# Chunk 0 and the tail of a recurrent-plus-experts kernel: some stores, a pair of sums, the later steps of three cells and three weight loads change place in an order written by hand

## The chip, the cores and the metric

The kernel runs on one core of a Trainium2 chip. A core has five engines that run side by side: TensorE (PE in the profile; its weight loads have a row of their own, PEld), VectorE (DVE), ScalarE (ACT), GpSimdE (POOL) and SyncE (SP), which here only issues transfers (DMAs). Each engine takes its own instructions strictly in the order in which the program issued them, so an instruction that has to wait holds up all that stand behind it on that engine. The metric is the time of one execution in microseconds (us), as the median of several runs; less is better.

## The reference, cut to what matters

The input x has 8 x 1024 tokens of 512 numbers, all float32. One layer is computed:

```
xn = layernorm(x)                                    # 8192 x 512
# a gated linear recurrence over the 1024 tokens of each sequence
hidden, forget, input = split(xn @ W1 + b1, 3)       # 1024 wide each
diff  = softplus(-forget) - softplus(-input)
h_t   = sigmoid(diff) * g(hidden_t) + sigmoid(-diff) * h_(t-1)   # the reference in logs: cumsum, cumlogsumexp
s     = h @ W2 + b2
# feed-forward: one shared expert, and one of 32 routed experts for each token
shared = (silu(xn @ sg) * (xn @ su)) @ sd
e      = argmax(xn @ gate_w);  score = sigmoid(max(xn @ gate_w))
routed = (silu(xs @ G[e]) * (xs @ U[e])) @ D[e]      # xs = xn * score, inner width 1024
out    = x + s * silu(shared + routed)
```

Here g(z) is z + 0.5 for z of at least 0 and sigmoid(z) below.

## The kernel before, in words

**Two stages.** The first stage goes over the tokens in 16 chunks of 512 and computes the recurrence, the shared expert and the choice of expert. What belongs to a token is written to two tables in memory: `rec1` holds xn times score, `rec2` holds x, the recurrence's output and the shared expert's output. The second stage goes over the 32 experts, gathers each expert's tokens from these tables, computes the routed expert and stores the result.

**Products by Strassen's scheme.** A chunk has 20 jobs (`JOBS`): for four pairs of column blocks the projections f, i, h (forget, input, hidden) of the recurrence and g, u (gate, up) of the shared expert. Each job is a product of a 512 x 256 weight block with the 512 tokens of the chunk, made of seven half-size products P1 to P7 (`multiply`, line 762 holds the matmul) instead of eight. For that it needs four sums of weight blocks, S1 to S4 (slots 0 to 3 of the tile `sums`), and four sums of token blocks (`t_sum`). P5 uses S1, P6 uses S2, P7 uses S3, P3 uses S4. S2 = S1 - A11 and S4 = A12 - S2 depend on each other; S3 = A11 - A21 stands alone. In chunk 0 (jobs 0 to 19) the sums are computed by `combine`, S1 and S4 on GpSimdE (lines 641 and 645), S2 and S3 on VectorE (lines 643 and 647), and then `save` (line 650) stores them to memory, 512 KB for each job. Later chunks only fetch them again (line 656). The tile `sums` has three buffers, `natural` (the weight block itself, loaded at line 594) has four.

**Banks.** P5 starts in a PSUM bank that ScalarE copies out (tag `p5`, line 776); P3 then adds onto the same bank, four places later. In the same way P6 adds onto P1's bank after P1's copy, P7 after P6's and P4 after P7's, each five places later. P2's bank and P5's bank are two that change roles from job to job. The copies are ScalarE instructions at lines 776 and 778, and pairs of them are added (`join`, line 788) by VectorE or GpSimdE.

**An order written by hand.** The first stage runs under a manual schedule. `now` counts slots; one slot issues one of the seven products of the current jobs, in the order P1, P4 of two jobs before, P5, P7 of the job before, P2, P6, P3. Everything else is put down with `at(slot, ...)` and is issued when the counter comes to that slot, after the slot's product. A slot is therefore a place in each engine's queue, not a time. From chunk 1 on, the products of the chunk before with W2 and sd (line 1058, "fills") are put between the others; chunk 0 has none.

**Cells.** A `Cell(c, p)` takes the f, i, h of one pair and does the elementwise part of the recurrence in 17 steps: absolute values, exponentials and logarithms on ScalarE (slots 24 to 31 after the job's start), `difference`, `less` and `more` on VectorE (32 to 34; lines 840, 844, 848), two gates on ScalarE (36 and 37; line 851, which need what `more` wrote), `sigmoid` and `positive` (39, 40), `value`, `weighed` and two scans on VectorE (42 to 47). There are four cells for each chunk.

**The second weights.** `out_sum` forms four sums of the weights W2 and of sd on VectorE (line 954) and stores each to a place in memory called `tdram` (line 958); `out_fetch` loads these or the plain blocks for the fills (lines 988 and 991).

**Prep.** For each chunk `Prep` loads x, normalises it, and `scale` (line 560) multiplies by the score; its store to `rec1` is line 561.

**The hand-over.** After the last product of the last chunk only its fills are left, 112 of them, two for each P1 to P7 and column half: this is the tail. `Dispatch` has by then made a table of which token goes where. In the tail the integer table `idx` is written, `numbers` loads the table again in two halves of four small transfers (line 1340), and VectorE turns each half into row numbers (line 1341) from which the later gathers of the experts start. The first expert's three weight blocks of 2 MB, e_wg, e_wu and e_wd, are loaded by `chunks[0].weight` (line 193): "g" ahead of the tail, "u" after 12 of its slots and "d" after 28. All these transfers stand in SyncE's one queue, and the built program gives them eight semaphores in turn, so that a transfer is issued only when the one eight places ahead of it has landed.

Of the kernel before, what the change touches and what calls it, by code (L numbers as in the profile page):

```python
# [17 lines left out]
P = 128  # L18
# [15 lines left out]
def tile_kernel(  # L34
# [45 lines left out]
    nc = tc.nc  # L80
# [24 lines left out]
    rec1 = dram.tile([N + 1, H], FP, name="rec1")  # L105
    rec2 = dram.tile([N + 1, 3 * H], FP, name="rec2")

    def work(name):
# [11 lines left out]
        out=upper, in_=ones, pattern=[[1, P]], compare_op=ALU.is_gt, fill=0.0,  # L120
# [42 lines left out]
    def expert(where):  # L163
        e = nc.values_load(
            where, engines=[ET.SP], min_val=0, max_val=E - 1,
            skip_runtime_bounds_check_because="the numbers of experts, or a count of them, clamped",
        )
        return [w[bass.ds(e, 1)].rearrange("o a b -> (o a) b") for w in (rgate_w, rup_w, rdown_w)]
# [207 lines left out]
    def alloc2(shape, tag, name):  # L376
# [4 lines left out]
    chunks = [  # L381
        Chunk(
            alloc2, alloc_w, f"e{e}",
            lambda t, e=e: pools["idx"][:, e * CT + t : e * CT + t + 1],
            lambda t, b, e=e: pools["fours"][:, b, e * CT + t : e * CT + t + 1],
            WIDTHS[e], lambda e=e: expert(eid[0:1, e : e + 1]), e == 0, e == E - 1,
        )
        for e in range(E)
    ]
# [3 lines left out]
    NP = DI // (2 * P)  # L393
# [32 lines left out]
    now = 0  # L426
    steps = {}

    def at(slot, what, *args):
        assert slot >= now  # L430
        steps.setdefault(slot, []).append(lambda: what(*args))
# [3 lines left out]
    class Prep:  # L435
# [121 lines left out]
        def scale(self, t):  # L557
            i = self.c * NT + t
            xn = self.xs.pop(t)
            nc.vector.tensor_scalar(xn, xn, self.sc[:, t : t + 1], None, ALU.mult)  # L560
            at(now + 2, lambda: nc.sync.dma_start(out=rec1[i * P : (i + 1) * P, :], in_=xn))

        def plan(self, g):

            g += 50 if self.c == 1 else 0
            for t in range(NT):
                at(g + 2 + 2 * t, self.load, t)
                at(g + 16 + 2 * t, self.stats, t)
                at(g + 32 + 2 * t, self.normal, t)
                at(g + 35 + 2 * t, self.store, t)  # L570
                at(g + 43 + 2 * t, self.pieces, t)
                at(g + 50 + 2 * t, self.turn, t)
                late = 70 if self.c == NCHUNK - 1 else 0
                at(g + 72 + late + 2 * t, self.again, t)
                at(g + 86 + late + t, self.scale, t)
            at(g + 12, self.keep)
            at(g + 24, self.variance, 0, NT)
            at(g + 28, self.spread, 0, NT)
            at(g + 66, self.router)
            at(g + 72, self.logits)  # L580
            at(g + 76, self.choose)
            at(g + 80, self.score)
# [77 lines left out]
    for n in range(NJOB):  # L660
        if n >= 3:
            at(7 * (n - 2) + 2, load, n)
        if n >= JC:
            at(7 * (n - 2) + 4, fetch, n)
        else:
            for q, s in ((0, 1), (2, 3), (1, 5), (3, 8)):
                at(7 * max(n - 1, 0) + s, combine, n, q)
            at(max(7 * n + 4, 10), save, n)

    tsum = {}  # L670

# [140 lines left out]
    class Cell:  # L812
# [66 lines left out]

        def plan(self):  # L880
            g = SC * self.c + 7 * JOBS.index((self.p, "f"))
            for slot, what, *args in (
                (24, self.size, "f", "d"), (25, self.exp, "lf"), (26, self.size, "i", "m"),
                (28, self.exp, "li"), (29, self.log, "lf"), (31, self.log, "li"),
                (32, self.difference), (33, self.less), (34, self.more),
                (36, self.gate, "i", 1.0), (37, self.gate, "f", -1.0),
                (39, self.sigmoid), (40, self.positive),
                (42, self.value), (43, self.weighed), (45, self.scan, 0), (47, self.scan, 1),
            ):
                at(g + slot, what, *args)  # L890

    class Hidden:

# [41 lines left out]
    def out_tile(name):  # L935
        return op.tile([P, NP, HC], FP, tag="wo", name=name, bufs=3)
# [10 lines left out]
    def out_sum(half, q):  # L947
        B11, B12, B21, B22 = out_blks[half][:4]
        l, r = {
            1: lambda: (B12, B11), 3: lambda: (B22, B12),  # L950
            2: lambda: (B22, out_blks[half][4]), 4: lambda: (B21, out_blks[half][5]),
        }[q]()
        o = out_tile(f"ot{half}_{q}")
        nc.vector.tensor_tensor(o, l, r, ALU.subtract)
        if q in (1, 2):
            out_blks[half].append(o)
        d = tdram[half, q] = dram.tile([P, NP * HC], FP, name=f"tdram{half}_{q}")
        at(now + 3, lambda: nc.sync.dma_start(out=d[:, :], in_=o.rearrange("p q f -> p (q f)")))

    for half, (a, b) in enumerate(((6, 18), (14, 40))):  # L960
        for k in range(4):
            at(a + 2 * k, out_load, half, *divmod(k, 2))
        for k, q in enumerate((1, 2, 4, 3)):
            at(b + 5 * k, out_sum, half, q)
# [6 lines left out]
    def out_fetch():  # L971

        u, name = next(out_next, (None, None))
        if u is None:
            return
        half = u[1]
        if "far" in pools:
            turn = next(far_turn)
            if turn % 5 < 2:
                o = pools["far"].tile([P, NP, HC], FP, tag="far", name=f"far{turn}")  # L980
            else:
                o = out_tile(f"w{name}_{half}")
            out_w[u, name] = o
        else:
            o = out_w[u, name] = out_tile(f"w{name}_{half}")
        if name in ("P1", "P2", "P3"):
            k, m = {"P1": (0, 0), "P2": (1, 0), "P3": (1, 1)}[name]
            nc.sync.dma_start(out=o, in_=out_block(half, k, m))
        else:
            q = {"P5": 1, "P6": 2, "P7": 3, "P4": 4}[name]  # L990
            nc.sync.dma_start(out=o.rearrange("p q f -> p (q f)"), in_=tdram[half, q][:, :])
# [20 lines left out]
    for c in range(NCHUNK):  # L1012
        g = SC * (c + 1)
        fast = c == NCHUNK - 1
        for p in range(NP):
            for q in range(1, 5):
                if p == NP - 1:
                    slot = (1, 2, 4, 6)[q - 1]
                else:
                    slot = (110, 112, 122, 132)[q - 1] + p - SC  # L1020
                at(g + slot, out_combine, c, 0, q, p)
                if fast:
                    slot = (20, 22, 26, 30)[q - 1] + p // 2
                else:
                    slot = (42, 44, 52, 61)[q - 1] + p
# [356 lines left out]
    d = Dispatch()  # L1382
# [36 lines left out]
    def due(slot):  # L1419

        c, s = divmod(slot, SC)
        if c == 0:
            return 0
        s -= 1
        if c == NCHUNK:
            return int(2 * (c - 1) * PER + min(max(RATE * s, 0), 2 * PER))
        part = min(max(s / 62, 0), 1) + min(max((s - 62) / 74, 0), 1)
        return int((2 * (c - 1) + part) * PER)
# [3 lines left out]
    for now in range(END):  # L1432
        name, back = ORDER[now % 7]
        n = now // 7 - back
# [25 lines left out]
    pools["far"] = c1.enter_context(tc.tile_pool(name="far", bufs=2, side="right"))  # L1460
    for _ in range(2):
        out_fetch()
    chunks[0].weight("g")
    k = 0
    while filled < 2 * NCHUNK * PER:
        now += 1
        for step in steps.pop(now, ()):
            step()
        while filled < due(now):
            next(fill)  # L1470
            filled += 1
        k += 1
        if k in (12, 28):
            chunks[0].weight("ud"[k // 28])
        if filled >= 2 * NCHUNK * PER - 24 and "xsT" not in vars(chunks[0]):
            pools["work"] = ps_w
            for t in range(CT):
                chunks[0].transpose(t)
# [50 lines left out]
    with tc.tile_pool(name="wo", bufs=3) as wo, tc.tile_pool(name="so", bufs=3) as so:  # L1529
        n = nc.values_load(  # L1530
            nov[0:1, 0:1], min_val=0, max_val=MAXOV,
            skip_runtime_bounds_check_because="a sum of at most MAXOV comparisons of counts that sum to N",
        )
# [56 lines left out]
```

## Time and profile before

| | |
|---|---|
| median of 3 runs | 4281.0 us (4280.41 to 4290.57) |
| the profiled execution itself | 4241.17 us |
| its span, first to last instruction | 4239.4 us |
| mean granted TensorE clock | 0.997 |
| TensorE busy | 4191.6 us, 99% |
| VectorE, ScalarE, GpSimdE busy | 2108.4, 1998.3, 1105.1 us |
| moved by DMA | 925.63 MB, 218 GB/s on average |

The profile shows one execution. Its timeline view lists instructions of an engine with start, length, line, output and inputs; a bracket at the end says how long the engine stood idle before, and which instruction of which engine ended that wait. The view of waits sums the same by pairs. Tensors carry the names of the program without buffer numbers. SPq is SyncE's queue of transfers.

### The profile page before, as it was taken

The numbers are of one execution on the slowest core, as the hardware profiler recorded it, in microseconds if no ns is written. First come the engines' busy times: TensorE is split into PE (matmuls) and PEld (weight loads), VectorE is DVE, ScalarE is ACT, GpSimd is POOL, SyncE is SP. The second block draws the span as 40 slices with busy tenths as digits, with TensorE's granted clock in tenths as the row PEclk, the third lists the DMA queues.
The fourth block names the chain that finished last, engine by engine and source line by source line (L and its number), as shares of the span: only waits on it lengthen the run. The fifth ranks groups of instructions, "written<-read, shape, count | busy, mean of one in ns | idle before, by whom it ended". The sixth has DMA issues, their size and how long they took to land.

```text
span 4239.4 us, 52532 instructions
## 1 busy us (share of the span) xinstructions
PE 4191.6 (99%) x18923; PEld 3568.1 (84%) x18923; DVE 2108.4 (50%) x3483; ACT 1998.3 (47%) x3662; POOL 1105.1 (26%) x1171
## 2 busy tenths in 40 slices
PE   8999999999999999999999999999999999999998
PEld 6888888888888888888888888866777788889998
DVE  6646454554554545555554456424444444544444
ACT  5676676666676767667666666500111111111111
POOL 3322112121221122212211125342232333333221
PEclk9999999999999999999999999999999999999999
DMA  7776666676676766766666666585666667677773
GB/s 261 234 225 224 214 218 212 204 230 209 210 223 210 227 207 206 229 210 215 216 211 220 207 191 199 168 290 178 213 225 224 210 233 243 220 252 244 242 264 114
DMA packets 507240, 925.63 MB, mean 218 GB/s; under 512 B 38397, under 2 KB 325021, under 8 KB 498786
## 3 DMA queue, kind: packets, MB, share of 16 engines
q1 hardware_dynamic: 479394, 832.27, 59.4%
q0 software_dynamic: 27584, 89.98, 6.4%
q8 instruction: 151, 2.47, 0.2%
q14 instruction: 111, 0.91, 0.1%
HBM read 805.27 MB, written 134.92 MB: 222 GB/s over the span
## 4 chain that ended last, share of the span: by engine, by line
PE 95%; DVE 2%; ACT 1%; issue 1%; DMA 1%; SPq 0%; POOL 0%; POOLq 0%; DVEq 0%; ACTq 0%
PE b L762 24%; PE u L1058 18%; PE c L762 12%; PE e_g L272 11%; PE e_u L272 11%; PE acc L261 11%; PE a L762 6%; PE b L713 0%; PE lgp L521 0%; DMA wP<-tdram 0%; DVE d L848 0%; DVE h L873 0%; DVE d L840 0%; PE lgt L531 0%; PE b L728 0%
## 5 line engine op out<-in xcount | busy, mean ns | idle before, releaser
L762 PE MATMUL b<-t,sums 128*128 128x256 f32 x2536 | 651.2, 379 | 2.2 <-DVE t L682 1.5
L1058 PE MATMUL u<-wP,s 128*128 128x256 f32 x2032 | 596.3, 379 | 2.4 <-issue 2.0
L277 ACT ACTIVATE e_sig<-e_g 128x280 f32<-128x280 f32 (+15 forms) x256 | 101.8, 398 | 933.4 <-PE e_g L272 933.3
L762 PEld LDWEIGHTS b<-t,sums 128*128 128x128 f32 x2536 | 480.6, 190 | 68.6 <-issue 1.9
L272 PE MATMUL e_g<-e_xsT,e_wg 128*128 128x296 f32 (+15 forms) x2048 | 518.0, 396 | 0.0
L272 PE MATMUL e_u<-e_xsT,e_wu 128*128 128x296 f32 (+15 forms) x2048 | 518.0, 396 | 0.0
L261 PE MATMUL acc<-e_h,e_wd 128*128 128x296 f32 (+15 forms) x2048 | 512.7, 396 | 0.0
L272 PEld LDWEIGHTS e_g<-e_xsT,e_wg 128*128 128x128 f32 x2048 | 389.1, 190 | 87.1
L272 PEld LDWEIGHTS e_u<-e_xsT,e_wu 128*128 128x128 f32 x2048 | 389.2, 190 | 87.0
L261 PEld LDWEIGHTS acc<-e_h,e_wd 128*128 128x128 f32 x2048 | 389.2, 190 | 87.0
L1058 PEld LDWEIGHTS u<-wP,s 128*128 128x128 f32 x2032 | 385.8, 190 | 57.0 <-issue 5.0
L279 DVE TENSOR_TENSOR e_sig<-e_sig,e_g 128x280 f32<-128x280 f32 (+15 forms) x256 | 113.3, 442 | 482.6 <-ACT e_sig L277 482.2
L762 PE MATMUL c<-xnT,sums 128*128 128x256 f32 x1268 | 326.8, 380 | 13.9 <-ACT p L776 13.5
L762 PE MATMUL b<-t,nat 128*128 128x256 f32 x1268 | 327.5, 381 | 0.0
L762 PE MATMUL b<-xnT,nat 128*128 128x256 f32 x1268 | 327.5, 381 | 0.0
L762 PE MATMUL c<-t,sums 128*128 128x256 f32 x1268 | 326.1, 380 | 0.0
L762 PE MATMUL a<-xnT,nat 128*128 128x256 f32 x1268 | 325.5, 379 | 0.1
L213 POOL DMA_INDIRECT e_xs<-rec,fours x276 | 261.8, 949 | 179.9 <-DMA e_rest<-rec,idx 80.2
L360 POOL DMA_INDIRECT out_dram<-e_rest,idx x84 | 93.2, 1110 | 801.8 <-DVE e_rest L359 798.9
L762 PEld LDWEIGHTS c<-xnT,sums 128*128 128x128 f32 x1268 | 240.3, 190 | 49.9 <-issue 14.0
L762 PEld LDWEIGHTS b<-t,nat 128*128 128x128 f32 x1268 | 242.6, 191 | 33.4
L762 PEld LDWEIGHTS b<-xnT,nat 128*128 128x128 f32 x1268 | 242.0, 191 | 33.5 <-issue 0.5
(245 smaller groups left out, 6298.9 us busy)
## 6 DMA issues: line engine op xcount, KB each, us to landing
sums<-sdram SPq DMA_DIRECT2D x300, 512.0 KB, 4.8
nat<-in_L_attn_W_dram SPq DMA_DIRECT2D x192, 512.0 KB, 4.6
e_wg<-L_ffn_routed_gate_w_dram SPq DMA_DIRECT2D x32, 2048.0 KB, 8.4
e_wu<-n_L_ffn_routed_up_w_dram SPq DMA_DIRECT2D x32, 2048.0 KB, 11.3
e_wd<-L_ffn_routed_down_w_dram SPq DMA_DIRECT2D x32, 2048.0 KB, 19.0
wP<-tdram SPq DMA_DIRECT2D x127, 512.0 KB, 4.3
nat<-L_ffn_shared_gate_w_dram SPq DMA_DIRECT2D x64, 512.0 KB, 4.7
nat<-n_L_ffn_shared_up_w_dram SPq DMA_DIRECT2D x64, 512.0 KB, 4.4
```

Source lines behind the costliest of these rows:

```text
L213: nc.gpsimd.indirect_dma_start(out=r[:, b, :], out_offset=None, in_=rec1.rearrange("n (a d) -> (n a) d", a=NA), in_offset=bass.IndirectOff ...
L261: nc.tensor.matmul(accs[m][:, :W], lhsT=wd[:, j, m * P : (m + 1) * P], rhs=h[:, :W], start=(j == 0), stop=(j == NI - 1),)
L272: nc.tensor.matmul(o[:, :W], lhsT=w[:, k, j * P : (j + 1) * P], rhs=xsT[:, k, :W], start=(k == 0), stop=(k == KH - 1),)
L277: nc.scalar.activation(sig[:, :W], g[:, :W], AF.Sigmoid)
L279: nc.vector.tensor_tensor(sig[:, :W], sig[:, :W], g[:, :W], ALU.mult)
L360: store = nc.gpsimd.indirect_dma_start(out=of[:, :], out_offset=bass.IndirectOffsetOnAxis(ap=col[:n, :], axis=0), in_=o, in_offset=None, b ...
L762: nc.tensor.matmul(ps, lhsT=lhs[:, k, :], rhs=rhs[:, k, :], start=(new and k == 0), stop=(k == KQ - 1),  skip_group_check=True,)
L1058: nc.tensor.matmul(ps[:, q, :], lhsT=lhs[:, q * P : (q + 1) * P], rhs=w[:, p, :],  start=(q == 0 and p == 0 and name in ("P1", "P2", "P5") ...
```

## The change

Six places of the hand-written order change; no instruction is added or taken away, and the products of TensorE keep their order.

- The store of `scale` to `rec1` is issued six slots after the multiplication instead of two (all chunks).
- In chunk 0, S2 is formed two slots earlier, S4 two slots earlier and ahead of S3, which comes five slots later; `save` is issued three slots later.
- The steps of cells 0 to 2 of chunk 0 that come after slot 31 (from `difference` on) are put two slots later. Cell 3 of chunk 0 and all later chunks keep their slots.
- The stores to `tdram` are issued nine slots after the sum instead of three.
- In the tail, the first expert's "g" weights are asked for after 10 slots instead of ahead of it, "u" after 20 instead of 12, "d" after 32 instead of 28. In the built program "g" then stands behind all eight transfers of `numbers`, and "d" behind one more store of the last results.

```diff
         def scale(self, t):
...
-            at(now + 2, lambda: nc.sync.dma_start(out=rec1[i * P : (i + 1) * P, :], in_=xn))
+            at(now + 6, lambda: nc.sync.dma_start(out=rec1[i * P : (i + 1) * P, :], in_=xn))
...
-            for q, s in ((0, 1), (2, 3), (1, 5), (3, 8)):
+            for q, s in ((0, 1), (1, 3), (3, 6), (2, 8)):
                 at(7 * max(n - 1, 0) + s, combine, n, q)
-            at(max(7 * n + 4, 10), save, n)
+            at(max(7 * n + 7, 13), save, n)
...
         def plan(self):
             g = SC * self.c + 7 * JOBS.index((self.p, "f"))
+            late = 2 if self.c == 0 and self.p < NP - 1 else 0
             for slot, what, *args in (
...
             ):
-                at(g + slot, what, *args)
+                at(g + slot + (late if slot > 31 else 0), what, *args)
...
-        at(now + 3, lambda: nc.sync.dma_start(out=d[:, :], in_=o.rearrange("p q f -> p (q f)")))
+        at(now + 9, lambda: nc.sync.dma_start(out=d[:, :], in_=o.rearrange("p q f -> p (q f)")))
...
     for _ in range(2):
         out_fetch()
-    chunks[0].weight("g")
     k = 0
     while filled < 2 * NCHUNK * PER:
...
         k += 1
-        if k in (12, 28):
-            chunks[0].weight("ud"[k // 28])
+        if k in (10, 20, 32):
+            chunks[0].weight("gud"[k // 10 - 1])
```

## The prediction

> **What bounds the kernel now.** I read the page first, then TensorE's waits, then the timelines of the places where it waits, then the order of the instructions in the two builds. The page:
>
> ```profile
> PE 4191.6 (99%) x18923; PEld 3568.1 (84%) x18923; DVE 2108.4 (50%) x3483; ACT 1998.3 (47%) x3662; POOL 1105.1 (26%) x1171
> ```
>
> TensorE is the bound nearly everywhere, so only stretches where it stands still can give time back. They lie in chunk 0 and at the hand-over to the experts. TensorE's waits of the first 220 us (total, times, longest), then lines of its timeline there (start, length; the wait before it in brackets):
>
> ```profile
> PE c L762 <- ACT p L776: 13.5, 7, 3.4
> PE b L762 <- DVE sums L643: 0.6, 2, 0.4
> PE c L762 <- POOL sums L645: 0.4, 1, 0.4
> ```
>
> ```profile
> 55.94 1.03 PE L762 MATMUL b<-t,sums 128*128 128x256 f32 x4
> 60.36 1.66 PE L762 MATMUL c<-xnT,sums 128*128 128x256 f32 x4 [3.40 <-ACT p L776]
> 61.81 1.91 PE L762 MATMUL b<-xnT,nat 128*128 128x256 f32 x4
> ...
> 76.62 1.10 PE L762 MATMUL c<-xnT,sums 128*128 128x256 f32 x4 [2.24 <-ACT p L776]
> ...
> 119.19 1.10 PE L762 MATMUL c<-xnT,sums 128*128 128x256 f32 x4 [1.65 <-ACT p L776]
> ...
> 155.09 1.10 PE L762 MATMUL c<-xnT,sums 128*128 128x256 f32 x4 [1.92 <-ACT p L776]
> ```
>
> The product waiting is always P3, four slots behind P5 in the same bank, held until ScalarE has copied P5 out. A product of four records starts every 0.865 us (43.36 to 44.22). Against that pace the gaps cost: 2.30 (at 50.7), 3.56 (60.4), 2.40 (76.6), 1.17 (102 to 104, two waits for sums), 1.19 (111.3), 1.82 (119.2), 1.33 (146.9), 2.09 (155.1). After three of them the records take 1.9 instead of 1.0: half clock for about 3.4 us, 1.75 each (155.09 to 160.30 is 5.21 for four products, 3.46 at pace). With 0.1 at 84.6 that is 21.2 us.
>
> The gaps are of two kinds. At 50.7, 76.6, 111.3 and 146.9 ScalarE is busy without a break: two exponentials, a table load of 1.28, a logarithm of 1.15, then the copy. At 60.4, 119.2 and 155.1 it stands before a gate (line 851) that waits for VectorE, with the copy queued behind. ScalarE, then VectorE:
>
> ```profile
> 54.04 1.28 ACT L851 ACT_TABLE_LOAD   x1
> 58.90 1.06 ACT L851 ACTIVATE i<-d 128x1024 f32<-128x1024 f32 x1 [3.58 <-DVE d L848]
> 59.87 0.35 ACT L776 COPY p<-c 128x256 f32<-128x256 f32 x1
> ```
>
> ```profile
> 51.98 1.22 DVE L840 TENSOR_TENSOR d<-d,m 128x1024 f32<-128x1024 f32 x1 [2.34 <-ACT m L836]
> ...
> 55.13 1.74 DVE L954 TENSOR_TENSOR ot<-wo,wo 128x1024 f32<-128x1024 f32 x1
> ```
>
> VectorE idles 2.34 before line 840, then runs other work between 840 and 848. At the hand-over (SyncE's waits, then TensorE's and VectorE's timelines):
>
> ```profile
> SPq L1340 <- DMA e_wg<-L_ffn_routed_gate_w_dram: 5.6, 1, 5.6
> ```
>
> ```profile
> 2769.43 3.69 PE L1058 MATMUL u<-wP,s 128*128 128x256 f32 x16 [0.37 <-DMA wP<-tdram]
> 2775.14 3.69 PE L1058 MATMUL u<-wP,s 128*128 128x256 f32 x16 [2.02 <-issue]
> ```
>
> ```profile
> 2772.68 0.41 DVE L1341 TENSOR_SCALAR fours<-number,piece 128x372 int32<-128x372 f32 x1 [1.26 <-DMA number<-table]
> 2773.01 1.42 DVE L1010 TENSOR_TENSOR s<-sh,s 128x256 f32<-128x256 f32 x4
> 2774.35 0.68 DVE L1070 TENSOR_TENSOR o<-u,a 128x512 f32<-128x512 f32 x1
> ```
>
> The 2 MB of e_wg, issued at 2753.94, hold up the numbers; VectorE waits for these, so line 1070 empties its bank only at 2775.03, and P5 starts at 2775.14. At a unit's pace of 3.46 the two gaps cost 0.53 and 2.25, together 2.78.
>
> **The change, part by part.** *Cells 0 to 2 of chunk 0, later steps two slots on.* Nothing is added. In the new order P5's copy and P7's eviction stand ahead of the table load and the gate, so P3 no longer waits for VectorE; P2's copy and P6's eviction are now behind the gate, with five slots' grace instead of four. In cell 0, VectorE does the ot of line 954 in its idle 2.34 (its inputs are there, and the store that frees its buffer leaves about 39.5 as before). Then, from 52.25, when the copy of P2 is out: join, 840, 844, join, cast, difference, 848. Those seven take 4.7 us start to start alone and 6.8 if each runs beside GpSimdE (0.42 becomes 0.95 and 1.21 becomes 1.74 in this trace); I take 5.8, which gives the gate at 58.1 instead of 58.90. TensorE wins 3.56 there, but ScalarE still owes the same work: from the gate on it needs 5.9 us of starts (0.97 for a big one, 0.25 to 0.36 for an eviction) to cell 1's first step, which begins at 64.0 instead of 67.02, and from there to P3 it is 9.6 us as now. So the 76.6 gap grows and 3.0 us remain. Cell 1's gate costs nothing now and little then (my count puts its P3 0 to 0.4 late). In cell 2 the copy of P5 is out 2 us early, nothing else is late by five slots: 1.8 gained.
>
> *S4 ahead of S3 (20 combinations of each kind).* No instruction more. Cell 3's steps are not moved, but one subtraction (0.34 start to start) leaves the place between lines 840 and 844, and S4 on GpSimdE, which began at 150.01 right behind it and lay beside two VectorE instructions (0.53 each), comes earlier. That is 0.3 to 1.4 off the gate's wait; I take 1.1, leaving a gap of about 1.0. The waits for sums (1.17) go too, at no gain: in the same cell ScalarE's unbroken chain sets P3's start, and the 1.19 at 111.3 becomes 2.36.
>
> *The clock.* The 1.92 gap in cell 3 was followed by half clock, 1.75; no gap of 1.65 or less in this trace was. Here a rule speaks against me: the Trainium skill, "TensorE: Matmul & The Clock Gate", Part 1, has the clock halve only after an idle window of about 3.4 us. By it neither 1.92 nor 2.24 could have halved it, and a shorter gap in cell 3 would save nothing more (sum 8.7). The rows of 1.9 us behind both gaps are there, so I go by them; but a gap of 2.14 at 50.7 was not punished, so the phase of a window matters, and a new half-clock stretch of 1.75 may appear in cell 2, where the gap grows to about 2.2.
>
> *Stores issued later: 20 saves of 512 KB, 8 tdram stores of 512 KB, 64 rec1 stores of 256 KB.* Same number, same bytes. SyncE now finds most of them ready: waits of 26 (line 650), 25 (958) and 14 us (561) in the first 250 us go, and loads queued behind leave up to 4 us sooner. TensorE waits for none of those loads (no nat in its list), so I book zero. The cover is their lead: load of job n at slot 7n-12, first product at 7n. From below, an earlier load could help the idle 1.35 before line 647 at 49.22, already counted as idle; from above, the sums ring, next paragraph but one. In chunk 1 three x loads now stand behind rec1 stores and wait for a landing (4.9 median); behind them is a load with 12 slots to spare, about 15 us.
>
> *Tail.* e_wg, e_wu, e_wd (three transfers of 2 MB) move behind the eight numbers, the last one also behind a store that waits for line 1081. Numbers then land by about 2766, line 1070 runs when P2 ends at 2769.1, and both gaps go: 2.78, taken as 2.8. What is late next: e_wd, issued about 2785.7 instead of 2775.55 and needed at 2797.8. The page's e_wg, alone in its queue, lands in 8.4; so 3.7 us of cover, and each us beyond costs one. GpSimdE's gathers are not moved.
>
> Sum: 3.0 + 1.8 + 1.1 + 1.75 + 2.8 = 10.45, say 10.5. The profiled execution took 4241.2 (span 4239.4); so 4230.7 for such a one. The median of the runs is 4281.0, 39.8 above, which no view explains; I take the saving over unchanged: 4270.5, 0.25% less. About 0.3%, 12.8 us, is what a measurement of this kernel can tell from no change.
>
> **The rivals.**
> *The gates run dry.* VectorE meets no GpSimdE work: cell 0's gate at 57.2 (4.1 gained, not 3.0), cell 3's as soon as its table is loaded at 151.4 (2.2, not 1.1), and the longer gap in cell 1 splits over P7, P2 and P3 so that its half clock goes too (1.75). 14.4 gained: 4266.6. For it: the copies that blocked are provably out of the way. Against: GpSimdE's S4 and S1 do fall between 52 and 56.
> *ScalarE takes it back.* Cell 0's gate at 58.9 as now: 1.9 left at P3 of cell 1; cell 3 unchanged; a new half clock in cell 2 (minus 1.75 from 1.8). With the tail 4.75: 4276.2.
> *Slower: the ring of three sums.* S1 of job n writes the buffer that save n-3 reads. Saves go three slots later and S2 two earlier, so from save to S2 there are 10 slots instead of 15: 8.65 us less S1's 0.9, so 7.8. If a save takes longer, S2 blocks VectorE, then the gates and joins. Each us beyond, over 14 jobs, is up to 14 us: slower than before from a lag plus landing of about 8.6, by over 0.3% from 9.5. Example at 10: 31 lost, 20 slower, 4301. Against: saves land in 5.5, at most 5.6, and no longer wait in the queue.
> That the change does nothing is excluded: the built order shows the moves.
>
> **How the numbers follow.** Forecast 0.46, gates run dry 0.36 (faster by over 0.3%), ScalarE takes it back 0.09, sums ring 0.09 (slower by over 0.3%). So faster 0.36, same 0.55, slower 0.09. The range runs from just beyond the dry gates (4265.0) to just beyond ScalarE's case (4277.5); the sums ring and what lies past the ends is left out.
>
> **What would show it.** Right: no P3 wait near 56 to 60 or 117 to 119; the wait near 73 longer, 3 to 4 us; a wait under 1.5 in cell 3 with full clock behind; no TensorE wait from 2760 to 2790; P3 of cell 1 about 3 us sooner. Wrong: new waits of SyncE on SBUF buffers, S1 waiting for a save, e_wd landing after 2797, half clock in new places, or waits of P5 and P2 for copies behind the gate.

## The result, and the profile after

| | before | after |
|---|---|---|
| median of 20 runs each | 4288.94 us (4280.41 to 4292.41) | 4281.51 us (4274.56 to 4284.88) |
| ratio | 1 | 0.9982, 95% interval 0.9975 to 0.9989 |
| profiled execution (span) | 4241.17 (4239.4) | 4284.2 (4282.5) |

The kernel became faster by 0.18%: 7.4 us between the medians, 4.7 to 10.7 by the interval. That is within 0.3%, as forecast, but the saving is smaller than the 10.5 predicted, and both times lie higher than the three runs shown ahead of the prediction said. The profiled execution of after is 43 us longer than that of before, although the change shortens the program. In the experiments this level of time went with the chip and not with the change.

Some readings of the profile of after answer to those shown of before. (In after, lines behind 881 have moved down by one: 1058 is now 1059, 954 is 955.) First, TensorE's waits of the first 220 us (total, times, longest):

```profile
PE c L762 <- ACT p L776: 9.8, 7, 2.4
...
PE b L762 <- DVE sums L647: 1.1, 2, 0.7
...
PE b L762 <- ACT u L776: 0.4, 1, 0.4
PE b L762 <- DVE rs L458: 0.3, 1, 0.3
```

The waits for P5's copy fell from 13.5 to 9.8. A wait that did not exist before is there: 1.1 for line 647, which is S3. TensorE's timeline says where (start, length; the wait before it in brackets):

```profile
56.19 1.03 PE L762 MATMUL c<-xnT,sums 128*128 128x256 f32 x4
...
63.47 1.10 PE L762 MATMUL c<-xnT,sums 128*128 128x256 f32 x4 [0.30 <-ACT p L776]
...
73.20 2.04 PE L762 MATMUL c<-xnT,sums 128*128 128x256 f32 x4 [2.40 <-ACT p L776]
...
97.31 1.10 PE L762 MATMUL b<-t,sums 128*128 128x256 f32 x4 [0.69 <-DVE sums L647]
...
99.58 1.10 PE L762 MATMUL b<-t,sums 128*128 128x256 f32 x4 [0.30 <-DVE rs L458]
...
131.69 1.10 PE L762 MATMUL b<-t,sums 128*128 128x256 f32 x4 [0.40 <-DVE sums L647]
...
151.47 1.10 PE L762 MATMUL c<-xnT,sums 128*128 128x256 f32 x4 [1.58 <-ACT p L776]
152.41 1.03 PE L762 MATMUL b<-xnT,nat 128*128 128x256 f32 x4
```

The wait of 3.40 in cell 0 is gone (56.19 has no bracket). Cell 3's is 1.58 instead of 1.92, and the product behind it takes 1.03: full clock. P7 now waits for S3 at 97.31 and 131.69; in before its products at the same two places did not wait. Second, ScalarE at cell 0's gate:

```profile
55.16 1.28 ACT L851 ACT_TABLE_LOAD   x1
57.62 1.06 ACT L851 ACTIVATE i<-d 128x1024 f32<-128x1024 f32 x1 [1.18 <-DVE d L848]
```

The gate begins at 57.62 instead of 58.90 (this execution began 0.61 earlier). It still waits 1.18 for VectorE, but P5's copy no longer stands behind it: it now stands ahead of the table load. Third, the tail:

```profile
2771.87 13.98 PE L1059 MATMUL u<-wP,s 128*128 128x256 f32 x64
2785.69 3.62 PE L1059 MATMUL u<-wP,h 128*128 128x256 f32 x16
2789.14 7.07 PE L1059 MATMUL u<-far,sh 128*128 128x256 f32 x32
```

The waits of 0.37 and 2.02 are gone, and from the start of the first stage's last product (line 762) to the first expert's first one it takes 44.61 us (2770.15 to 2814.76) instead of 47.48 (2742.99 to 2790.47): 2.87 less.

**Product by product.** Set side by side by order, with the 0.61 of the start taken off, the products of after stand ahead of those of before by the following (by the time of before):

| at, us | 60.4 | 76.6 | 90.7 | 111.3 | 119.2 | 125.3 | 135.1 | 155.1 | 170.2 |
|---|---|---|---|---|---|---|---|---|---|
| after | 3.56 | 2.81 | 3.13 | 2.15 | 3.97 | 3.13 | 2.75 | 3.01 | 4.69 |

Together with the tail that is 7.56, against 7.4 us between the medians and 7.7 by the ratio: these two places account for the result.

### The profile page after: what moved, and what is told of

Same layout as the page of the kernel before. It is cut to its first block, busy times and chain, and to the rows that moved or that the text cites. A ratio compares the mean times of both kernels' runs of the same rounds, so it can differ in the third digit from the quotient of the medians.

```text
span 4282.5 us, 52548 instructions
## 1 busy us (share of the span) xinstructions
PE 4203.1 (98%) x18923; PEld 3569.7 (83%) x18923; DVE 2111.2 (49%) x3483; ACT 1999.2 (47%) x3662; POOL 1103.3 (26%) x1171
## 4 chain that ended last, share of the span: by engine, by line
PE 94%; DVE 2%; ACT 2%; issue 1%; DMA 0%; another core or an unknown queue 0%; SPq 0%; POOL 0%; POOLq 0%; DVEq 0%; ACTq 0%
PE b L762 24%; PE u L1059 18%; PE c L762 12%; PE acc L261 11%; PE e_g L272 11%; PE e_u L272 11%; PE a L762 6%; PE b L713 0%; PE lgp L521 0%; DVE h L873 0%; ACT L836 0%; PE lgt L531 0%; DVE d L840 0%; ACT L832 0%
## 5 line engine op out<-in xcount | busy, mean ns | idle before, releaser
L762 PEld LDWEIGHTS c<-t,sums 128*128 128x128 f32 x1268 | 241.1, 190 | 39.9 <-issue 7.1
```

The costliest lines, as they stand in the source:

```text
L762: nc.tensor.matmul(ps, lhsT=lhs[:, k, :], rhs=rhs[:, k, :], start=(new and k == 0), stop=(k == KQ - 1),  skip_group_check=True,)
```

## Experiments

Kernels that were run together shared one chip and its runs of before. The first four share one chip, the next four a second, the rest a third. "Ahead" is the lead over before at the end of chunk 0 (170 us), with the start taken off.

**Before once more.** No edit.

> The kernel before, unchanged, profiled and timed once more. What is open: the execution profiled before took 4241.2 while the median of its runs is 4281 to 4289, and the execution profiled after took 4284.2, with some 41 us of standstill in the second stage (PE waits of 5 to 12 us named 'issue' between 2590 and 2850, VectorE and ScalarE standing too) in places that the change does not touch. Theory L (luck of one execution): the change has no part in these; a second profile of before shows waits named 'issue' of 10 to 45 us in the second stage and a span of 4275 to 4290, and the ratio is 1.000. Rival C (the change causes them): this profile is again near 4240, with PE's 'issue' waits in the second stage under 5 us, and then the median of before cannot be explained by them.

Measured: 4288.78 (ratio 1.0006, 0.9998 to 1.0014), its profile 4279.34. The waits are there, so the change has no part in them:

```profile
PE acc L261 <- issue: 12.7, 1, 12.7
...
PE b L762 <- issue: 2.9, 1, 2.9
PE u L1058 <- issue: 2.6, 1, 2.6
PE a L762 <- issue: 2.3, 1, 2.3
PE c L762 <- issue: 1.7, 1, 1.7
```

But luck of one execution is not the answer either. The four kernels "stores alone", "S3 first", "cell 3 late too" and "both" below fell on another chip, where before took 4240.83 in 55 runs (4238.12 to 4242.8), and outside chunk 0 and the tail none of their four profiles has a wait of TensorE above 1.55 us. So, as far as three chips show, the level, 4241 or 4287, belongs to the chip. Chunk 0, equal in both programs, came out 0.29 ahead here and 0.02 behind in the next experiment's: so much is noise of one execution.

**The tail's weights alone.**

```diff
-    chunks[0].weight("g")
...
-        if k in (12, 28):
-            chunks[0].weight("ud"[k // 28])
+        if k in (10, 20, 32):
+            chunks[0].weight("gud"[k // 10 - 1])
```

> The weights of the tail alone (g after 10 slots, u after 20, d after 32). Theory: TensorE's waits of 0.37 and 2.02 near 2769 and 2775 go, the stretch from the first tail fill to the first product of the first expert falls from 52.7 to 49.8 us; time 2.8 less than before, ratio 0.9993. Rival 'e_wd late': the first down product waits for e_wd, gain under 1, ratio 0.9998 or more. Chunk 0 as before.

Measured: ratio 0.9986 (0.9978 to 0.9994); from the first stage's last product to the first expert 44.60 us against 47.45 in the repeat of before on the same chip, which is 2.85. The predicted 2.8 is right, and belongs to this edit alone. The rival came in a small part: the first down product waits for e_wd, and starts 10.37 behind the first gate product instead of 10.10.

**The later steps alone.**

```diff
+            late = 2 if self.c == 0 and self.p < NP - 1 else 0
...
-                at(g + slot, what, *args)
+                at(g + slot + (late if slot > 31 else 0), what, *args)
```

> Only the later steps of cells 0 to 2 two slots on, chunk 0; sums, saves, stores and tail as before. Theory A (the moved sums cost what is missing): cell 0 and 1 gain 3.0 to 3.1 at the P3 near 90, cell 2 gains 1.5 to 2 more at the P3 near 135, because S3 comes in time; then chunk 0 ends 4.6 to 5.1 earlier, cell 3 as before with its wait of 1.9 and the half clock behind; ratio 0.9989. Rival B (cell 2 loses by itself: the longer chain on ScalarE takes it back): cell 2 gains under 0.5, chunk 0 ends 2.9 to 3.5 earlier; ratio 0.9993.

Measured: ratio 0.9995 (0.9988 to 1.0002), 2.17 ahead. Both theories fall. It leads by 2.37 at 90.7, by 3.61 at cell 2's gate (119.2) and by 3.28 at 135.1, more than after there; then it loses nearly all of it. S2 and S4 come late in cells 2 and 3:

```profile
100.44 1.10 PE L762 MATMUL b<-t,sums 128*128 128x256 f32 x4 [1.64 <-DVE sums L643]
...
101.94 1.13 PE L762 MATMUL c<-xnT,sums 128*128 128x256 f32 x4 [0.40 <-POOL sums L645]
...
137.49 1.69 PE L762 MATMUL c<-xnT,sums 128*128 128x256 f32 x4 [1.41 <-POOL sums L645]
138.97 1.91 PE L762 MATMUL b<-xnT,nat 128*128 128x256 f32 x4
```

The first two waits cost little: behind them P3 of the same cell, which is held up by ScalarE's copy, waits 0.27 instead of 1.02, and from 90.7 to 111.3 the lead falls by 0.6 (in after by 1.0). The third does cost: with two short waits ahead of it (0.49 and 0.71) it brings half clock, from 137.92 to 141.33, and the lead goes from 3.28 to -1.16 (142.5). What comes back by 146.9, to 0.17, is a wait of before (1.17) that falls away here. At 155 it is 0.49 ahead, and 1.68 more comes from the half clock of before that stayed away there. So the earlier S4 is what keeps the later steps' lead in cell 3; how much of the loss would remain without the half clock was not tried.

**The sums alone.**

```diff
-            for q, s in ((0, 1), (2, 3), (1, 5), (3, 8)):
+            for q, s in ((0, 1), (1, 3), (3, 6), (2, 8)):
                 at(7 * max(n - 1, 0) + s, combine, n, q)
-            at(max(7 * n + 4, 10), save, n)
+            at(max(7 * n + 7, 13), save, n)
```

> Only the order of the sums (S4 ahead of S3, S3 five slots later) and the saves three slots later, chunk 0. Theory A (late S3 costs): P7 waits for S3 on VectorE in cells 2 and 3, 0.3 to 0.7 each time and 1.5 together, against 0.35 at the gate of cell 3 and at most 1.75 of half clock behind it: chunk 0 ends 0 to 0.6 earlier if the half clock goes, 0.5 to 1.5 later if not; ratio 0.9999 to 1.0003. Rival B (the reordering gains, as predicted 1.1 + 1.75): chunk 0 ends 2 to 3 earlier, no P7 wait for S3; ratio 0.9994. Saves: no wait of S1 for a save in either.

Measured: ratio 0.9997 (0.9989 to 1.0006), 2.18 ahead: 0.49 at 155 and 1.69 by the clock behind a gap of 1.59. P7 waits for S3 only once, 0.20. Between the theories: the reordering gains a third of a microsecond at the gate of cell 3, not 1.1, and late S3 costs little while the cells' steps stand where they were. No S1 waited for a save.

**Stores alone** (`rec1` six slots behind, `tdram` nine).

> The kernel before with only the stores to rec1 (six slots behind instead of two) and to tdram (nine instead of three) issued later. Theory: nothing moves on TensorE, chunk 0 ends within 0.3 of before net of the start, the tail keeps its 47.5 us, ratio 1.000. Rival: earlier loads or later stores matter, chunk 0 or the tail differs by 0.5 or more.

Measured: ratio 0.9998 (0.9990 to 1.0007), 2.21 ahead. Of that, 0.52 appears at the first gate: with the stores out of the way the load of a weight block leaves sooner, S1 runs at 44.52 instead of 49.32, GpSimdE is done with its block of work before the gate, and VectorE's S2 there takes 0.42 instead of 0.95. The other 1.69 is the clock: here the same gap of 1.92 in cell 3 was not followed by half clock (see the last section). The tail took 48.91, 1.4 longer, with a half-clock stretch behind its gap of 2.38. The run of the sums alone, whose tail is that of before too, also took 48.91, with half clock from 2803.23; so the tail's edit takes away the chance of this as well. The theory of zero holds to half a microsecond, and the rival for that half.

**S3 first.** After, with one more edit:

```diff
-            for q, s in ((0, 1), (1, 3), (3, 6), (2, 8)):
+            for q, s in ((0, 1), (2, 2), (1, 3), (3, 6)):
```

> The changed kernel with one more edit: in chunk 0 the sum S3 is formed first of VectorE's two, six slots earlier than in the changed kernel (it needs only the weight block); S2, S4, saves, cells as changed. Theory A (S3's place cost the missing time: VectorE runs without a break from about 86 to 102 and 119 to 138, and S3 stood at the end of that queue): P7's waits for S3 at 97 and 131 go, chunk 0 ends 1.0 to 1.6 earlier than in the changed kernel, that is 5.7 to 6.3 ahead of before, net of the start. Rival B (VectorE is simply full there, another product waits instead, for S2 or S4 or a t sum): chunk 0 ends within 0.4 of the changed kernel. In ratio to before A gives 0.9979, B 0.9982.

Measured: ratio 0.9979 (0.9972 to 0.9986), 4.94 ahead. The waits for S3 are gone, but the rival is right that VectorE is full. S2 now stands last in its queue; TensorE waits for it, and half clock follows:

```profile
100.85 1.14 PE L762 MATMUL b<-t,sums 128*128 128x256 f32 x4 [1.93 <-DVE rs L458]
101.79 2.04 PE L762 MATMUL c<-xnT,sums 128*128 128x256 f32 x4
103.62 1.81 PE L762 MATMUL b<-xnT,nat 128*128 128x256 f32 x4
```

The release is named after a small instruction of VectorE (line 458) that directly follows S2 at 100.28 to 100.70. The kernel "both" has the same order up to here and the same wait, 1.82, without half clock behind it; at 125 it leads by 4.61 instead of 2.74, and after by 3.13. So S3's place was worth 1.5 at that point (4.61 less 3.13), unless the clock takes 1.87 back. The wait for S2 by itself costs nothing: at 111.3 "both" leads by 3.29 with it, and the version further down that has no such wait by 3.32. ScalarE's chain sets P3's start there.

**Cell 3 late too.** After, with `late = 2 if self.c == 0 else 0`.

> The changed kernel with the later steps of cell 3 of chunk 0 two slots on as well. Theory A: the wait of P3 at 151.5 (1.58 behind ScalarE's gate) goes as it did in cells 0 and 2; chunk 0 ends 1.0 to 1.8 earlier than in the changed kernel. Rival B: ScalarE or VectorE hand it back at the end of the chunk, where chunk 1 begins with its fills: under 0.5 earlier. Ratio to before 0.9979 by A, 0.9982 by B.

Measured: ratio 0.9990 (0.9983 to 0.9996), 3.75 ahead: worse than after by 0.9, of which 0.5 arises in cell 3; the other 0.4 arises ahead of the edit, where P7's wait for S3 happened to take 0.96 instead of 0.69. The 1.58 goes, as theory A has it, but right behind it TensorE waits 1.28 for a copy of ScalarE (at 154.83) and 0.22 more at 159.13. The rival is right, and more than it said.

**Both.** S3 first and cell 3 late.

> Both further edits together (S3 first, and cell 3 late too). Theory A, the two add up: chunk 0 ends 2.0 to 3.4 earlier than in the changed kernel, 6.7 to 8.1 ahead of before; ratio to before 0.9976. Rival B, they share one limit (VectorE's queue): no more than the better of the two, 1.0 to 1.8; ratio 0.9979.

Measured: ratio 0.9980 (0.9972 to 0.9988), 6.60 ahead. Against S3 first alone all of the difference is the half clock that this execution escaped in cell 2; in cell 3 the one goes from 2.92 to 4.94, the other from 4.79 to 6.60. The two edits do not add up.

**After once more.** No edit to after.

> The changed kernel, unchanged, profiled and timed once more, beside its further versions. From the traces so far: chunk 0 ends 4.7 ahead of before net of the start and the tail is 2.87 shorter, 7.6 together; ratio 0.9982. What varies between executions is the half clock: TensorE's clock halves for the next 3.41 us where it stands idle for about 1.9 or more of one window of 3.41 in a grid that lies differently in each execution. Expected: half clock behind cell 1's gap of 2.40 and in no other place of chunk 0, chunk 0 4.4 to 5.0 ahead; a second level of time (near 4235 or near 4281) decided by the chip the run is on, with before at 4241 or 4287 beside it.

Measured: 4281.91, ratio 0.9987 (0.9978 to 0.9995), 4.87 ahead, tail 44.61, half clock in chunk 0 behind cell 1's gap alone: as expected.

**VectorE's load taken out of the way.** S3 first, and for chunk 1 the loads of x and the statistics (lines 454 and 455, four pairs of 0.87) six slots earlier:

```diff
+                early = 6 if self.c == 1 else 0
-                at(g + 2 + 2 * t, self.load, t)
-                at(g + 16 + 2 * t, self.stats, t)
+                at(g + 2 - early + 2 * t, self.load, t)
+                at(g + 16 - early + 2 * t, self.stats, t)
```

> The changed kernel with S3 formed first (six slots earlier) and, for chunk 1 alone, the four x loads and the four statistics of the normalisation six slots earlier, so that VectorE does their 3.5 us in its idle gaps between 81 and 86 instead of in the unbroken stretch from 87 to 102. Theory A (VectorE's load sets cell 2's loss): no TensorE wait at 97 to 100 of more than 0.5, S2 is ready some 2 to 3 us sooner, chunk 0 ends 1.0 to 2.0 earlier than with S3 first alone where that had no half clock (net 6.7), that is 7.5 to 8.7 ahead of before; ratio 0.9974. Rival B (ScalarE's unbroken chain takes it back at the gap near 107, which grows from 0.3 to 1.7 or more): no more than 0.5 over 6.7; ratio 0.9978. Rival C: the earlier loads wait for their five buffers and hold up SyncE's queue: TensorE waits for a weight block near 70 to 80, slower than the changed kernel.

Measured: ratio 0.9966 (0.9955 to 0.9977) over only seven runs, 6.84 ahead. S2's wait at 100 is gone, and so is the chance of half clock there. But ScalarE takes the rest back, as rival B says; P3's wait for it in cell 2 is 1.64 instead of 0.27. The same kernel a second time:

> The version with S3 first and chunk 1's statistics early, timed and profiled once more, because its first seven runs fell from 4283 to 4268 in their order and its ratio of 0.9966 is more than its trace gives. From the trace: chunk 0 ends 6.8 ahead of before net of the start, the tail is 2.87 shorter, 9.7 together: ratio 0.9977. If the ratio is again 0.997 or less, something outside chunk 0 and the tail is faster by 3 or more; if it is 0.9974 to 0.9980, the first ratio was its seven runs' own. Half clock in chunk 0: once, behind cell 1's gap of 2.40.

Measured: ratio 0.9976 (0.9968 to 0.9985), 7.00 ahead, tail 44.60. TensorE's waits in cells 2 and 3 there (lines have moved by one: 762 is 763, 645 is 646, 776 is 777):

```profile
98.74 1.13 PE L763 MATMUL c<-xnT,sums 128*128 128x256 f32 x4 [0.39 <-POOL sums L646]
...
106.70 1.10 PE L763 MATMUL c<-xnT,sums 128*128 128x256 f32 x4 [1.65 <-ACT p L777]
...
148.69 1.10 PE L763 MATMUL c<-xnT,sums 128*128 128x256 f32 x4 [1.58 <-ACT p L777]
```

The trace gives 7.00 and 2.85, that is 9.85, or 0.9977: the second ratio agrees, the first was its seven runs' own. This version beats before clearly. That it beats after, by 2.1 us (means of two profiles each), rests on the traces: the intervals of its first ratio and of after's on the same chip do not meet (0.9955 to 0.9977 and 0.9978 to 0.9995), but those of the second ratio and of the result above do.

**The same with cell 3 late.**

> As the version with the statistics early, and cell 3's later steps two slots on as well. Theory A: cell 3's P3 wait (1.58) goes for good because VectorE and ScalarE have less behind them: 0.8 to 1.6 beyond the version with the statistics early. Rival B: as in the two versions with cell 3 late so far (1.28 for a copy, 0.94 for S4 in its place): within 0.4 of it.

Measured: ratio 0.9976 (0.9967 to 0.9984), 6.79 ahead: rival B again, with 0.94 for S4 in place of 1.58 for the copy.

## Why the prediction was right or wrong

Two things were wrong. The time came out 11.0 us above the 4270.5 predicted. Of this 7.9 is the base, 4281.0 where 20 runs gave 4288.94. The other 3.1 is the saving, 10.5 where 7.4 came between the medians (7.56 by the trace). Its largest part is a step of the argument that failed: "nothing else is late by five slots: 1.8 gained" in cell 2. S3, which the change itself moved five slots on, was late, and the 1.8 came out as zero. The saving lies between the forecast and the rival "ScalarE takes it back" (4.75). Term by term:

**Cells 0 and 1: right.** Booked 3.0; the lead at the P3 behind cell 1's gate (84.6) is 3.06, one job later (90.7) 3.13, and there 3.36 in the repeat. The path was as told: 3.56 won at the gate, then part of it handed back through ScalarE. Only the form differs: the gap near 73 is 2.40, because small waits (0.30 at 63.47, 0.43 at 67.59) came before it. The 3 to 4 that was announced for it does not follow from the prediction's own sum, which gives 2.24 plus 0.56, that is 2.8.

**Cell 2: the step that failed first.** Booked 1.8, with "nothing else is late by five slots". The gate did give 1.82 (2.15 to 3.97). But S3, moved five slots later, was late. VectorE works without a pause from 86 to 102 in after, as it does from 88 to 103 in before; only, S3 stood near the start of that stretch and now stands late in it. Before, VectorE, TensorE and ScalarE:

```profile
90.91 0.85 DVE L647 TENSOR_TENSOR sums<-nat 128x256 f32<-128x256 f32 x1
...
100.16 1.03 PE L762 MATMUL b<-t,sums 128*128 128x256 f32 x4
...
101.28 0.47 ACT L778 ACTIVATE u<-b,vec 128x256 f32<-128x256 f32 x1 [0.50 <-PE b L762]
101.66 1.05 ACT L828 ACTIVATE d<-f 128x1024 f32<-128x1024 f32 x1
```

After, VectorE, then ScalarE:

```profile
95.03 1.28 DVE L873 TENSOR_TENSOR_SCAN h<-i,ginit,f 128x512 f32<-128x512 f32 x1
96.34 0.15 DVE L878 COPY carry<-h 128x1 f32<-128x1 f32 x1
96.41 0.42 DVE L788 TENSOR_TENSOR i<-c,u 128x256 f32<-128x256 f32 x1
96.75 0.42 DVE L647 TENSOR_TENSOR sums<-nat 128x256 f32<-128x256 f32 x1
97.08 0.69 DVE L454 BATCH_NORM_STATS2 st<-x 128x6 f32<-128x512 f32 x1
...
98.51 0.48 ACT L778 ACTIVATE u<-b,vec 128x256 f32<-128x256 f32 x1 [1.42 <-PE b L762]
98.88 1.05 ACT L828 ACTIVATE d<-f 128x1024 f32<-128x1024 f32 x1
```

No line of VectorE has a bracket. S3 ends at 97.17 and P7 starts at 97.31. ScalarE waits 1.42 for P7 before it evicts it (line 778), and right behind that begins cell 2's unbroken chain (line 828): at 98.88 instead of 101.66, which with the start taken off is a lead of 2.17 only. From 90.7 to 111.3 TensorE's lead falls from 3.13 to 2.15, the gate brings it to 3.97, and behind the gate 0.84 goes back, in waits for ScalarE's copies (125.3). Net zero instead of 1.8. In "both", with S3 first and no half clock in cell 2, the same stretch goes from 3.43 to 4.61. So 1.2 of the 1.8 were lost to S3's place; 0.6 stayed lost even so, 0.5 of it behind the gate.

**The order of the sums: wrong in size, with a cost that was not counted.** Booked 1.1 at cell 3's gate. The gate comes sooner by only 0.26 (2.75 to 3.01 in the lead; 0.35 in the wait). S4 was not beside VectorE any less: GpSimdE's S4 and S1 lie from 145.19 to 148.56, beside lines 840 and 844, which take 1.49 and 1.63 there; and the subtraction taken out was worth the 0.34 it was said to be. P7's second wait for S3 took 0.38 away again (3.13 to 2.75). The waits for sums of 1.17 "go at no gain": right for the place, but in cell 3 the later steps without the earlier S4 wait 1.41 for it and fall into half clock, as the run of those steps alone shows. The edits of chunk 0 were summed as if each stood alone. Alone, stores, later steps and sums lead by 0.5 each at 155 (the later steps after a half-clock stretch in cell 3); together by 3.0.

**The clock: right here, but not a sure gain.** Booked 1.75, measured 1.68 (3.01 to 4.69). The Trainium skill ("TensorE: Matmul & The Clock Gate", Part 1) puts the slow state after at least one idle window of about 3.4 us. Taken as the only way into it, as the prediction took it, that leaves no half clock behind 1.92 and nothing to win here; the rows decide against that reading. But the run with the stores alone was free of half clock in the same place with the same gap of 1.92, so the expected value of the step was under 1.75.

**Stores: booked zero**, measured 0.5 alone, and SyncE does not find the saves ready: its waits before line 650 in the first 250 us are 48 in after, 26 in before, and now nearly all for S3. Those before the stores to `tdram`, 25, did go; those before line 561 fell from 14 to 8. The sums ring, the rival that ends slower, did not come: no S1 waited for a save.

**Tail: right.** Booked 2.8, measured 2.87. The cover of 3.7 us for e_wd was wrong, because it took e_wd to land in the 8.4 of a transfer alone in its queue. In the run of the tail alone e_wd was issued at 2811.04 and the first down product's wait for it ended at 2823.18, 12.1 later; with S3 first it was 12.1 as well. That product comes 10.21 behind the first gate product in after instead of 10.10, and 10.3 to 10.7 in the profiles of the further versions: e_wd is late by 0.1 to 0.6. At the end no such loss is seen: from the first gate product on it takes 1449.0 with S3 first and 1448.8 in "both", against 1449.0 in before.

**The base: too low, by the luck of three runs.** The saving was taken off 4281.0, the median of three. Over 20 runs it was 4288.94; of the first three (4280.41, 4290.57 and 4281.0) two are the lowest of all 20. 10.5 off 4288.94 gives 4278.4; nearly all of the other 3.1 are the chunk-0 terms above, 7.65 booked against 4.69 (cell 2's 1.8, cell 3's gate 0.8, the second S3 wait 0.4).

## What to carry to other kernels

A sum of separately reasoned edits to a hand-written order is not safe when they stand in one engine's queue: ask of each moved instruction what is in front of it in its new place, and whether that engine has any pause there. VectorE at 50% of the span was full for 15 us just where it mattered. An operand that depends on nothing but a load can be formed first; here that was worth 1.2 us in cell 2 where no half clock followed. And when the level of a profile does not fit the median of the runs, look for stretches where several engines stand with no releaser, and do not take either number as a sure base.

## What the runs showed of the hardware

**The half clock goes by a fixed grid.** The stretches of half clock in one execution begin at multiples of 3.41 us from each other (in before 60.8, 77.8 and 156.3; so in all 14 profiles), and the grid lies differently in each execution. What counts is how long TensorE works in one window. Two windows each of before, of the stores alone, of S3 first and of S3 first with cell 3 late (stretch, its length, PE busy and records, PEld, DVE, ACT, POOL, then the granted clock, DMA share, GB/s):

```profile
152.93:156.34 3.41, 1.49 (x8) 1.15 (x7) 3.27 (x9) 2.71 (x6) 0.10 (x1) 1.00 0.78 221
156.34:159.75 3.41, 3.41 (x10) 2.66 (x9) 2.90 (x4) 3.27 (x8) 1.61 (x2) 0.50 1.05 411
```

```profile
153.50:156.91 3.41, 1.68 (x8) 1.52 (x9) 3.27 (x10) 3.14 (x7) 0.52 (x1) 1.00 0.79 250
156.91:160.32 3.41, 3.41 (x18) 3.00 (x17) 2.90 (x4) 3.30 (x8) 1.22 (x3) 1.00 1.05 405
```

```profile
98.37:101.78 3.41, 1.48 (x7) 0.86 (x6) 3.38 (x8) 3.38 (x5) 1.00 (x2) 1.00 0.33 114
101.78:105.19 3.41, 3.41 (x9) 2.78 (x9) 2.81 (x5) 2.02 (x4) 3.41 (x4) 0.50 0.41 159
```

```profile
96.46:99.87 3.41, 1.59 (x8) 1.11 (x7) 3.34 (x10) 2.90 (x5) 0.20 (x1) 1.00 0.45 154
99.87:103.28 3.41, 3.41 (x16) 2.88 (x17) 2.81 (x5) 3.40 (x7) 3.41 (x4) 1.00 0.41 155
```

Busy 1.49 and 1.48 of 3.41 halved the next window (x10 and x9 records instead of x18 and x16), 1.68 and 1.59 did not. The gap of 1.92 in the first two pairs is the same; in the second it reached over the border of a window. Laid over chunk 0 from 44 us on, in all 14 profiles, the grid has 17 windows with TensorE idle for 2.08 us or more, and half clock followed every one; with 1.82 or less it followed none. Of the ten between (1.86 to 1.99) five were followed by it; among the other five is the one of before around the gap of 2.14 at 50.7, with 1.99 idle. So the border is not sharp in these records. A gap of about 1.9 us brings half clock only if it falls inside one window: by an estimate from 3.41 and 1.92, (3.41 - 1.92) / 3.41, in 0.44 of the phases. The Trainium skill, in Part 1 of the page named above ("TensorE: Matmul & The Clock Gate"), states a free-running window of 3413 ns, which these 3.41 us agree with; that a partly idle window is enough is what the rows add.

**On some chips other engines stand still while GpSimdE issues indirect DMAs.** In every profile at the 4280 level ScalarE, VectorE and TensorE stand for 9 to 18 us at about 2830 while GpSimdE issues gathers. The repeat of before, GpSimdE's last gather, ScalarE, TensorE; then ScalarE at the same place in the profile of before at 4241:

```profile
2838.49 0.98 POOL L223 DMA_INDIRECT e_rest<-rec,idx  x1 [0.30 <-issue]
...
2828.18 0.48 ACT L277 ACTIVATE e_sig<-e_g 128x376 f32<-128x376 f32 x1 [11.99 <-remote]
2843.75 0.48 ACT L277 ACTIVATE e_sig<-e_g 128x376 f32<-128x376 f32 x1 [15.09 <-remote]
...
2843.51 4.85 PE L261 MATMUL acc<-e_h,e_wd 128*128 128x376 f32 x8 [12.68 <-issue]
```

```profile
2820.99 0.48 ACT L277 ACTIVATE e_sig<-e_g 128x376 f32<-128x376 f32 x1 [7.10 <-PE e_g L272]
2828.57 0.48 ACT L277 ACTIVATE e_sig<-e_g 128x376 f32<-128x376 f32 x1 [7.10 <-PE e_g L272]
```

The stall ends some 4 us behind GpSimdE's last gather (2839.5, then 2843.5 here). The same happens from about 2595 to 2690, where GpSimdE writes the table with 64 indirect DMAs. From the first expert's first product to the end it takes 1464.6 us in that repeat and 1448.9 in before's profile; the rest of the difference lies ahead of the tail. Half clock follows these stalls: between 2600 and 2850 the repeat has 34 us of it and before's profile none. By an estimate from half of 34 that is at most 17 of the 38 us between the two spans (4277.6 and 4239.4). Between the two levels nothing differs in the program, and GpSimdE's gathers take the same 30 us in both (2808.4 to 2838.5, and 2785.9 to 2815.9). Of the three chips of the experiments two did this in every profile and one in none. What the engines wait for was not tried and stays open, and so does whether the gathers cause it; the records name no releaser, and no packet that fetches instructions falls into the stretch from 2812 to 2850.
